# A graph attention layer on one core: the node phase's stores, the one-hot's place and the exponential steps

## The chip, the cores and the metric

The kernel runs on one core of a Trainium2 chip. The core has a matrix engine (TensorE, PE in the profile; PEld is its weight load), a vector engine (VectorE, DVE), a scalar engine (ScalarE, ACT), GpSimd (POOL) and a queue engine (SyncE, SP) that here only issues DMAs. The metric is the device time of one execution in microseconds (us); lower is better.

## The reference

There are 12500 nodes with 128 channels and 400000 edges, sorted by their target. What is computed:

```python
h = maximum(layernorm(x), 0)
msg_src = h @ w_src + b_src                    # per node
msg_dst = h @ w_dst
message = msg_src[edge_src] + msg_dst[edge_dst]   # per edge
rad_w = silu(silu(edge_attr_32 @ w1 + b1) @ w2 + b2) @ w3 + b3
message = message * edge_weight * rad_w
message = message @ w_sep + b_sep              # 8 heads of 16 alphas and 16 values
alpha, value = split(message)
score = einsum(smooth_leaky_relu(alpha), alpha_dot)       # per edge and head
att = segment_softmax(score, edge_dst)
out = segment_sum(value * att, edge_dst) @ w_proj + b_proj
return x + out
```

## The kernel before

**Node phase.** The nodes are taken in 25 groups, `Q`, twice. The first pass (`products(i, 0)`) makes rows `h @ w_src` and stores them to a table `t_src` in device memory; the second pass (`products(i, 1)`) makes `t_dst`. Between these products stand small jobs: layer norm statistics, the rows of the first five pairs (`raw_*`), and the loads of weights and of the first edges, which `weights_list()` hands to SyncE one or two at a time. `marks(j)` (L601) compares, on VectorE, each edge's target with the next one's and leaves a bf16 mark in `gt`; after the fourth quarter `same` is stored (L605 to L608), in device memory; later stages read it to see where a segment ends. Late in the second pass come the loads `load_d(0)`, `load_w(0)` and `load_w(1)`: targets and edge weights of the first pairs, into buffers of `messages`.

**Edge phase.** An edge section is 512 edges, and a *pair* is two sections, 1024 edges: 391 pairs. `windows()` runs `step(k)` for k = -5 to 390 and a tail; a step works on many pairs in different stages:

- GpSimd gathers the rows of `t_src` for pair k+2 with indirect DMAs of 128 rows (`gather`, L1111), eight per pair. The first five pairs are not gathered. GpSimd may run ahead of its step as far as buffers are free: pairs 5 to 12 go into `messages`, later ones into rotating buffers, six pairs deep (`gs`, `mT`, `xs`, `gu` are their names).
- The radial network runs three steps deep: `mlp1(k+2)` (PE L1127, ACT L1130, its two halves in the banks `m1` and `misc`), `mlp2(k+1)` (L1140, L1142), `mlp3(k)` (L1157) and `radial(k)` (DVE L1162, times the edge weight).
- `one_hot_T(k+1)` makes, on ACT (L1151, L1152), the one-hot of the targets, with which PE picks rows of `t_dst` (`md`, loaded by `load_md` at L1080, split by `split_md` into high and low parts on ACT L1090 and DVE L1094).
- `sources(k)` (PE L1173) transposes the gathered rows into the bank `pm`; `message(k)` (PE L1186) adds the target's part; DVE L1191 multiplies and leaves the message, `mT`.
- `alphas(k-1, f)` is PE's product L1197 and ACT's SiLU L1199, then DVE's L1204; `scores` (PE L1214, every second step) writes its result into `m1`.
- Every eighth step (k % 8 == 3, k = 11, 19, ... 387) is an *exponential step*: `softmax_exp` (ACT L1250) needs another function table in ACT than SiLU, so two table loads stand in it; `softmax_T` (PE L1284, ACT L1287) transposes the result through the bank `misc`.
- `values` (PE L1325, DVE L1327) and `sums` (PE L1340, L1352) work on pair k-12.

The order of the instructions on each engine is the order in which `step` calls these helpers; semaphores come from the framework's tracking of tiles. Each engine works its own list in order.

```python
for f in (1, 0):
    nc.scalar.activation(h1s[k][:, f, :], p1[f], AF.Silu, bias=b12[:, 0:1], scale=1.0)
```

Here `p1[0]` is `m1`, the bank that `scores` needs next in odd steps, and `p1[1]` is `misc`.

Of the kernel before, what the change touches and what calls it, by code (L numbers as in the profile page):

```python
# [42 lines left out]
KV = 320  # L43
MP = 8
# [3 lines left out]
AHEAD = 13  # L48
# [9 lines left out]
def gnn_kernel(ctx: ExitStack, tc: tile.TileContext, a: dict, out: bass.AP):  # L58
# [8 lines left out]
    NP = NS // 2  # L67
# [130 lines left out]
    with tc.tile_pool(name="node1", bufs=1) as n1, tc.tile_pool(name="node", bufs=2) as np_, \  # L198
# [80 lines left out]
        def weights_list():  # L279
# [10 lines left out]
            for f in range(2):  # L290
# [4 lines left out]
                for q in range(2):  # L295
# [4 lines left out]
                [lambda: load_d(0, early[AHEAD - 2].bitcast(I32).rearrange("p (n e) -> p n e", n=2)),  # L300
                 lambda: load_w(0, early[AHEAD - 3]), lambda: load_w(1, early[AHEAD - 1])]

# [334 lines left out]
        stats(*quads[4])  # L637
        roots(quads[3][0], quads[4][1])
        more = iter(weights_list())
        limits = load_limits()  # L640
        for i in range(Q):
# [31 lines left out]
            if i == 19:  # L673
                ends_load()
        extra = {7: lambda: (spans(), places()), 10: cuts, 12: direct_ids, 14: spreads,
                 15: lambda: marks(0), 16: lambda: marks(1), 18: lambda: marks(2), 20: lambda: marks(3)}
        for i in range(2 * RQ + 8):
            if i < Q:
                products(i, 1)
            if i % 2 == 0 and 0 <= i // 2 - 4 < RQ:  # L680
                raw_turn(i // 2 - 4)
            q = i // 2 - 1
            if i % 4 == 2 and q < RQ:
                raw_roots(q, q + 2)
            if i % 4 == 3 and q < RQ:
                raw_scales(q, q + 2)
            if i % 2 == 0 and 0 <= q - 1 < RQ:
                raw_norm(q - 1)
            if i in extra:
                extra[i]()  # L690
            load = next(more, None)
            if load:
                load()
            if i == 2 * RQ:
                nc.scalar.activation(silu, eps[0:1, :], AF.Silu)
# [313 lines left out]
    def windows():  # L1009
# [7 lines left out]
        with tc.tile_pool(name="ps", bufs=1, space=PSUM) as pp, \  # L1017
# [104 lines left out]
            def mlp1(k):  # L1122
# [5 lines left out]
                h1s[k] = sp.tile([P, 2, 2 * T], F32, name="h1")  # L1128
                for f in (1, 0):
                    nc.scalar.activation(h1s[k][:, f, :], p1[f], AF.Silu, bias=b12[:, 0:1], scale=1.0)  # L1130
# [506 lines left out]
            def has(k):  # L1637
                return 0 <= k < NP

            prep[0] = idx0  # L1640
            for k in range(2):
                load_md(k)

            def tail_head(c):
# [19 lines left out]
            def step(k):  # L1664
# [29 lines left out]
                if k % 16 == 7 and has(k + 9) and k > 7:  # L1694
                    prep_make((k + 9) // 16)
                if 0 <= k - 40 < 8:
                    padded_rows(k - 40)
                unit = k >= UNIT_STEP[0]
# [9 lines left out]
                if has(k + 1) and k >= 0:  # L1708
                    split_md(k + 1, 0)
                m, r = divmod(k, MP)  # L1710
                if k >= NP:
                    m, r = LAST_M + 1, k - NP
                if k == NP:
                    tail_head(c)
                    return
                if has(c):
                    weights(c)
                    values(c, 0)
# [10 lines left out]
                if has(k + 1) and k >= 0:  # L1729
                    split_md(k + 1, 1)  # L1730
                if has(k - 1):
# [6 lines left out]
                if has(k):  # L1738
                    mlp3(k)
                if has(k + 2):  # L1740
                    mlp1(k + 2)
                if has(k + 1):
                    one_hot_T(k + 1)
                if has(k):
                    radial(k)
                if k == 0:
                    for i in range(2):
                        split_md(0, i)
                if unit and q == 1:
# [29 lines left out]
                if has(k + 2):  # L1779
                    gather(k + 2, 1)  # L1780
                if has(k + 3):
                    e_T(k + 3)
# [10 lines left out]
                if has(k):  # L1793
                    message(k)
                if has(k - MP) and r == 3:
                    softmax_T(m - 1, 0)
# [229 lines left out]
```

## Time and profile before

| | |
|---|---|
| median of 3 runs | 4045.88 us (4044.23 to 4051.89) |
| profiled execution | 4045.58 us |
| its span, first to last instruction | 4043.7 us |
| mean granted TensorE clock | 0.974 |
| PE, DVE, ACT, POOL busy | 3734.2, 2966.2, 2317.5, 3015.5 us |

In the rows of a timeline the columns are the start in us, the duration in us, the engine, the line, the operation, output<-input tiles, and in brackets the idle time of the engine before it and what released it. In the rows of waits they are the total in us, the number of times and the longest. "issue" as a releaser means that the profile shows nothing that the engine waited for. SPq and POOLq rows are DMA issues. A granted clock of 0.50 means TensorE ran at half its speed in that stretch.

### The profile page before, as it was taken

What the parts mean: (1) busy time and instruction counts of PE and PEld (TensorE: products, weight loads), DVE (VectorE), ACT (ScalarE), POOL (GpSimd) and SP (SyncE); (2) the same over time, 40 slices, a digit from 0 to 9 for tenths busy, and PEclk for the clock granted to TensorE, in tenths of its full rate; (3) what the DMA queues carried; (4) which work ended last, traced back from release to release, by engine and by line L of the source; (5) the groups of instructions that cost most, each with busy time, mean ns of one, the idle gap of its engine ahead of it and who ended that gap; (6) DMA issues with size and microseconds to landing.
All of it is one profiled execution on the core that took longest, in us unless ns stands there. A gap on an engine that the chain in (4) does not pass through costs nothing. (4 is left out here: it accounts for less than half of the span.)

```text
span 4043.7 us, 82719 instructions
## 1 busy us (share of the span) xinstructions
PE 3734.2 (92%) x27186; PEld 2198.2 (54%) x27186; DVE 2966.2 (73%) x5236; ACT 2317.5 (57%) x4463; POOL 3015.5 (75%) x3193
## 2 busy tenths in 40 slices
PE   7699999999999999999999999999999999999997
PEld 6255555555555555555555555555555555565555
DVE  8477777777777767677777677777777777777876
ACT  7565555666655556555655565555555555555561
POOL 6767777777777777777777777777777777777776
PEclk9899999999999999999999999999999999999998
DMA  8756666666666665665566666666666666666662
GB/s 256 189 154 166 166 177 170 162 171 170 175 160 170 167 162 159 166 162 166 158 169 169 163 164 169 168 162 165 172 171 159 178 167 180 174 179 181 174 166 56
DMA packets 435839, 678.82 MB, mean 168 GB/s; under 512 B 96574, under 2 KB 268510, under 8 KB 435291
## 3 DMA queue, kind: packets, MB, share of 16 engines
q1 hardware_dynamic: 331931, 464.59, 39.4%
q0 software_dynamic: 101888, 207.34, 21.8%
q8 instruction: 220, 3.60, 0.4%
q14 instruction: 216, 1.77, 0.2%
q10 hardware_dynamic: 1584, 1.51, 0.1%
HBM read 620.73 MB, written 54.06 MB: 167 GB/s over the span
## 5 line engine op out<-in xcount | busy, mean ns | idle before, releaser
L1111 POOL DMA_INDIRECT gs<-t_src,idx x3013 | 2849.4, 946 | 932.4 <-issue 757.2
L1204 DVE SCALAR_TENSOR_TENSOR al<-pa,sl 128x512 f32<-128x512 f32 x781 | 538.9, 690 | 544.1 <-ACT sl L1199 533.2
L1197 PE MATMUL pa<-mT,c_w_a 128*128 128x512 f32 x1562 | 884.1, 648 | 38.7 <-DVE mT L1191 17.9
L1199 ACT ACTIVATE sl<-pa,c_b_a 128x512 f32<-128x512 f32 x781 | 536.8, 687 | 666.4 <-PE pa L1197 659.5
L1325 PE MATMUL V<-c_w_v,mT 128*128 128x128 f32 x6154 | 891.2, 288 | 11.4 <-DVE pvx L1327 10.7
L1325 PEld LDWEIGHTS V<-c_w_v,mT 128*128 128x128 f32 x6154 | 757.3, 194 | 240.9 <-issue 186.3
L1173 PEld LDWEIGHTS pm<-ident,gs 128*128 128x128 f32 x3013 | 374.5, 143 | 536.3 <-issue 526.3
L1142 ACT ACTIVATE h<-p,b 128x512 f32<-128x512 f32 x391 | 467.7, 1196 | 345.7 <-PE p L1140 339.5
L1327 DVE TENSOR_TENSOR pvx<-V,Pem 128x512 f32<-128x512 f32 x770 | 528.0, 686 | 146.4 <-PE V L1325 96.9
L1162 DVE SCALAR_TENSOR_TENSOR w_b<-p,c_fc_b,w_b 128x1024 f32<-128x1024 f32 x389 | 498.2, 1281 | 147.1 <-PE p L1157 119.7
L1173 PE MATMUL pm<-ident,gs 128*128 128x128 f32 x3013 | 464.3, 277 | 99.5 <-DMA gs<-t_src,idx 98.9
L1191 DVE SCALAR_TENSOR_TENSOR mT<-pm,c_b_src,w_b 128x1024 f32<-128x1024 f32 x389 | 495.6, 1274 | 14.8 <-PE pm L1186 14.5
L1130 ACT ACTIVATE h<-misc,b 128x256 f32<-128x256 f32 x391 | 185.6, 475 | 540.7 <-PE misc L1127 522.4
L1157 PE MATMUL p<-h,w3b 64*128 64x512 f32 x1564 | 454.9, 659 | 8.0 <-ACT h L1142 8.0
L1197 PEld LDWEIGHTS pa<-mT,c_w_a 128*128 128x128 f32 x1562 | 236.2, 191 | 288.3 <-issue 78.7
L1214 PE MATMUL m<-al,w_s 128*32 128x512 f32 x1564 | 215.8, 623 | 80.8 <-ACT h L1130 79.6
L1152 ACT ACTIVATE ohT<-d_b,ones 128x512 fp32r<-128x512 f32 x389 | 280.8, 722 | 13.0
L1151 ACT ACTIVATE d_b<-d_b,tgt 128x512 f32<-128x512 int32 x389 | 279.9, 719 | 0.0
L1140 PE MATMUL p<-h,w2b 64*64 64x256 f32 x3128 | 260.3, 403 | 0.0
L1127 PEld LDWEIGHTS m<-eT,w1b 64*128 64x128 f32 x782 | 151.0, 193 | 196.6 <-issue 169.9
L1127 PE MATMUL m<-eT,w1b 64*128 64x256 f32 x782 | 239.5, 387 | 3.9 <-DMA t_dst<-ms 2.7
L1127 PE MATMUL misc<-eT,w1b 64*128 64x256 f32 x782 | 239.5, 387 | 0.0
(257 smaller groups left out, 3730.3 us busy)
## 6 DMA issues: line engine op xcount, KB each, us to landing
w_b<-in_edge_weight SPq DMA_DIRECT2D x388, 512.0 KB
d_b<-in_dst SPq DMA_DIRECT2D x388, 256.0 KB
e_t<-in_edge_attr SPq DMA_DIRECT2D x381, 128.0 KB
gs<-t_src,idx POOLq DMA_INDIRECT x3013
md<-t_dst SPq DMA_DIRECT2D x782, 32.0 KB
win<-ob SPq DMA_DIRECT2D x230, 68.0 KB
agg<-ob SPq DMA_DIRECT2D x640, 16.5 KB
xs<-in_x SPq DMA_DIRECT2D x26, 256.0 KB
```

The lines of the kernel that those rows point to most:

```text
L1111: sent = [nc.gpsimd.indirect_dma_start(out=gs[:, t, :], out_offset=None, in_=t_src[:, :], in_offset=bass.IndirectOffsetOnAxis(ap=idx[:, t0 ...
L1127: nc.tensor.matmul(p1[f], w1b[s, :], eTs[k][s, :], start=True, stop=True)
L1142: nc.scalar.activation(h2s[k].rearrange("x (h i b) -> x h b i", h=2, b=2 * TS), p2[:, :, 0:2 * T].rearrange("x h (b i) -> x h b i", b=2 * TS),
L1157: nc.tensor.matmul(p3[:, f, 0:SEC], w3b[s, :], h2s[k][s, :], start=True, stop=True)
L1162: nc.vector.scalar_tensor_tensor(rad[:, 0:n], p3.rearrange("c f e -> c (f e)")[:, 0:n], b3, rad[:, 0:n], op0=ALU.add, op1=ALU.mult)
L1173: turned = [nc.tensor.matmul(pm[:, t * T:(t + 1) * T], gs[:, t, :], ident, start=(t == 0), stop=False, is_transpose=True, skip_group_check ...
L1191: nc.vector.scalar_tensor_tensor(mTs[k][:, 0:n], pms.rearrange("c f e -> c (f e)")[:, 0:n], b_n, rad[:, 0:n], op0=ALU.add, op1=ALU.mult)
L1197: nc.tensor.matmul(pa[:, 0:n], w_a, mTs[k][:, f * SEC:f * SEC + n], start=True, stop=True)
L1199: nc.scalar.activation(sl[:, 0:n], pa[:, 0:n], AF.Silu, bias=b_a, scale=1.0)
L1204: nc.vector.scalar_tensor_tensor(al, pa, 0.25, sl, op0=ALU.mult, op1=ALU.add)
L1325: nc.tensor.matmul(V[:, t, :], mTs[c][:, o:o + T], w_v, start=True, stop=True)
L1327: nc.vector.tensor_mul(pvx[c][:, f, 0:n, 0:C].rearrange("p t (h k) -> p t h k", h=H), V[:, 0:n, :].rearrange("p t (h k) -> p t h k", h=H), ...
```

## The change

Six things move; no operation of the computation is added or taken away.

1. `marks(0)` to `marks(3)`, and with them the stores of `same`, go from the second pass (groups 15, 16, 18, 20) into the last four groups of the first.
2. `load_w(1)`, the second pair's edge weights, goes from the node phase's list to just behind `load_md(0)` and `load_md(1)` at the start of `windows()`.
3. In odd `mlp1` up to pair 320, ACT reads `m1` first and `misc` second.
4. In step 0, pair 0's `split_md` stands where pair 1's stood, and pair 1's goes behind `message(0)`.
5. `one_hot_T(k+1)` goes from before `radial(k)` to behind the second `alphas` of the step.
6. In exponential steps `mlp1(k+2)` goes behind the second `alphas`, `sources` and `gather`.

Also, `padded_rows` is called in steps 40 to 51, two of every three, instead of 40 to 47. `raw_rows` is only a function around lines that were inline (its body and the removed lines are left out).

```diff
@@ -298,7 +298,7 @@
             return [lambda t=t, ap=ap: nc.sync.dma_start(out=t, in_=ap) for t, ap in pairs] + \
                 [lambda k=k: load_e(k, nc.sync) for k in range(4)] + \
                 [lambda: load_d(0, early[AHEAD - 2].bitcast(I32).rearrange("p (n e) -> p n e", n=2)),
-                 lambda: load_w(0, early[AHEAD - 3]), lambda: load_w(1, early[AHEAD - 1])]
+                 lambda: load_w(0, early[AHEAD - 3])]
 
 
         mv = n1.tile([P, NB, 3], F32, name="mv")
@@ -636,6 +636,18 @@
         stats(*quads[3])
         stats(*quads[4])
         roots(quads[3][0], quads[4][1])
...
         more = iter(weights_list())
         limits = load_limits()
         for i in range(Q):
@@ -672,20 +684,13 @@
                 ends_store()
             if i == 19:
                 ends_load()
-        extra = {7: lambda: (spans(), places()), 10: cuts, 12: direct_ids, 14: spreads,
-                 15: lambda: marks(0), 16: lambda: marks(1), 18: lambda: marks(2), 20: lambda: marks(3)}
+            if 0 <= i - (Q - 4) < 4:
+                marks(i - (Q - 4))
+        extra = {7: lambda: (spans(), places()), 10: cuts, 12: direct_ids, 14: spreads}
         for i in range(2 * RQ + 8):
             if i < Q:
                 products(i, 1)
...
+            raw_rows(i)
             if i in extra:
                 extra[i]()
             load = next(more, None)
@@ -1126,7 +1131,7 @@
                     s = slice(f * 2 * RAD, (f + 1) * 2 * RAD)
                     nc.tensor.matmul(p1[f], w1b[s, :], eTs[k][s, :], start=True, stop=True)
                 h1s[k] = sp.tile([P, 2, 2 * T], F32, name="h1")
-                for f in (1, 0):
+                for f in (0, 1) if k % 2 and k < KV else (1, 0):
                     nc.scalar.activation(h1s[k][:, f, :], p1[f], AF.Silu, bias=b12[:, 0:1], scale=1.0)
 
             def mlp2(k):
@@ -1640,6 +1645,7 @@
             prep[0] = idx0
             for k in range(2):
                 load_md(k)
+            load_w(1, early[AHEAD - 1])
 
             def tail_head(c):
 
@@ -1693,8 +1699,8 @@
                     prep_make(k // 2 - 1)
                 if k % 16 == 7 and has(k + 9) and k > 7:
                     prep_make((k + 9) // 16)
-                if 0 <= k - 40 < 8:
-                    padded_rows(k - 40)
+                if 0 <= k - 40 < 12 and (k - 40) % 3 != 1:
+                    padded_rows((k - 40) // 3 * 2 + (k - 40) % 3 // 2)
                 unit = k >= UNIT_STEP[0]
                 u = max((i for i, a in enumerate(UNIT_STEP) if a <= k), default=0)
                 q = k - UNIT_STEP[u]
@@ -1706,13 +1712,14 @@
                 if k % 16 == LAG - 1 and has(k - LAG + 1) and k < NP:
                     loc_turn(k // 16)
                 if has(k + 1) and k >= 0:
-                    split_md(k + 1, 0)
+                    split_md(k + (k > 0), 0)
                 m, r = divmod(k, MP)
                 if k >= NP:
                     m, r = LAST_M + 1, k - NP
                 if k == NP:
                     tail_head(c)
                     return
+                after = has(k - MP) and r == 3 and k < NP
                 if has(c):
                     weights(c)
                     values(c, 0)
@@ -1727,7 +1734,7 @@
                 if c - 2 >= D and has(c - 2):
                     direct_turn(c - 2)
                 if has(k + 1) and k >= 0:
-                    split_md(k + 1, 1)
+                    split_md(k + (k > 0), 1)
                 if has(k - 1):
                     alphas_sum(k - 1, 0, *sl)
                 j, o = divmod(k - LATE, SB)
@@ -1737,15 +1744,10 @@
                         block_exp(j)
                 if has(k):
                     mlp3(k)
-                if has(k + 2):
+                if has(k + 2) and not after:
                     mlp1(k + 2)
-                if has(k + 1):
-                    one_hot_T(k + 1)
                 if has(k):
                     radial(k)
-                if k == 0:
-                    for i in range(2):
-                        split_md(0, i)
                 if unit and q == 1:
                     unit_bias(u)
                     unit_quotients(u, sp)
@@ -1778,6 +1780,10 @@
                     sources(k, 1)
                 if has(k + 2):
                     gather(k + 2, 1)
+                if has(k + 2) and after:
+                    mlp1(k + 2)
+                if has(k + 1):
+                    one_hot_T(k + 1)
                 if has(k + 3):
                     e_T(k + 3)
                 if has(k - 1):
@@ -1792,6 +1798,9 @@
                     direct_out(c - 2)
                 if has(k):
                     message(k)
+                if k == 0:
+                    for i in range(2):
+                        split_md(1, i)
                 if has(k - MP) and r == 3:
                     softmax_T(m - 1, 0)
                 if has(k + 1):
```

Where it moves instructions, first on SyncE. Before, this is the end of its list for the node phase; `mT` are the buffers of `messages` that take targets and weights:

```order
L605 DMA same<-gt 96x3584
L605 DMA same<-gt 15x3584
L607 DMA same<-gt 1x2176
L608 DMA same<-past 1x1409
L175 DMA e_t<-in_edge_attr 128x256
L367 DMA t_dst<-ms_1223 128x1024
L187 DMA mT<-in_dst 64x2x512 x2
L194 DMA mT<-in_edge_weight 128x1024
L367 DMA t_dst<-ms_1257 128x1024
L194 DMA mT<-in_edge_weight 128x1024
L367 DMA t_dst<-ms_1282 128x128
L369 DMA t_dst<-ms_1282 84x128
```

After the change the same end reads as follows, in the same place:

```order
L367 DMA t_dst<-ms_1194 128x1024
L175 DMA e_t<-in_edge_attr 128x256 x2
L367 DMA t_dst<-ms_1228 128x1024
L187 DMA mT<-in_dst 64x2x512 x2
L194 DMA mT<-in_edge_weight 128x1024
L367 DMA t_dst<-ms_1257 128x1024
L367 DMA t_dst<-ms_1281 128x128
L369 DMA t_dst<-ms_1281 84x128
```

The four stores of `same` and one of the two weight loads are gone from it. The stores stand now between the last store of `t_src` and the first of `t_dst`, some thirty rows further up:

```order
L367 DMA t_src<-ms_872 128x128
L369 DMA t_src<-ms_872 84x128
L298 DMA c_fc_w_146<-in_fc_w 64x128
L605 DMA same<-gt 96x3584
L605 DMA same<-gt 15x3584
L607 DMA same<-gt 1x2176
L608 DMA same<-past 1x1409
L298 DMA c_fc_b_147<-in_fc_b 128x1
L367 DMA t_dst<-ms_888 128x1024
```

And the second pair's weights stand behind the `md` loads of pairs 0 and 1:

```order
L1082 TENSOR_LOAD base x2
L1085 ISA
L1085 DMA md<-t_dst 64x1x128
L1085 ISA
L1085 DMA md<-t_dst 64x1x128
L194 DMA mT<-in_edge_weight 128x1024
L1082 TENSOR_LOAD base x2
L1085 ISA
```

They are the next thing on SyncE after those four loads of `md`.

On ACT, an odd step of the first ten, before (`h` are `mlp1`'s halves, `d_b` and `ohT` the one-hot, `sl` the alphas' SiLU):

```order
L1199 ACTIVATE sl<-pa,c_b_a 128x512
L1130 ACTIVATE h_1718<-misc,b_131 128x256
L1130 ACTIVATE h_1718<-m_1333,b_131 128x256
L1151 ACTIVATE d_b<-d_b,tgt 128x512
L1152 ACTIVATE ohT<-d_b,ones 128x512
L1199 ACTIVATE sl<-pa,c_b_a 128x512
L1142 ACTIVATE h_1753<-p_1332,b_131 128x2x8x32
```

The same rows after:

```order
L1204 ACTIVATE sl<-pa,c_b_a 128x512
L1135 ACTIVATE h_1718<-m_1332,b_131 128x256
L1135 ACTIVATE h_1718<-misc,b_131 128x256
L1204 ACTIVATE sl<-pa,c_b_a 128x512
L1156 ACTIVATE d_b<-d_b,tgt 128x512
L1157 ACTIVATE ohT<-d_b,ones 128x512
L1147 ACTIVATE h_1753<-p_1331,b_131 128x2x8x32
```

The second `sl` is now ahead of the one-hot instead of behind it, and the half of `h` from the bank `m` is made first.

Step 19, an exponential step, on ACT, before (`Pr` is the exponential, `S` the scores' copy, `Pem` the transposes' copies):

```order
L1250 ACT_TABLE_LOAD
L1250 ACTIVATE Pr<-M 128x512
L1130 ACT_TABLE_LOAD
L1130 ACTIVATE h_2916<-misc,b_131 128x256
L1130 ACTIVATE h_2916<-m_1333,b_131 128x256
L1151 ACTIVATE d_b<-d_b,tgt 128x512
L1152 ACTIVATE ohT<-d_b,ones 128x512
L1218 ACTIVATE S<-m_1333,b_s 128x512
L1199 ACTIVATE sl<-pa,c_b_a 128x512
L1287 COPY Pem<-misc 128x256
L1142 ACTIVATE h_2964<-p_1332,b_131 128x2x8x32
```

And after:

```order
L1255 ACT_TABLE_LOAD
L1255 ACTIVATE Pr<-M 128x512
L1223 ACTIVATE S<-m_1332,b_s 128x512
L1204 ACT_TABLE_LOAD
L1204 ACTIVATE sl<-pa,c_b_a 128x512
L1135 ACTIVATE h_2943<-m_1332,b_131 128x256
L1135 ACTIVATE h_2943<-misc,b_131 128x256
L1156 ACTIVATE d_b<-d_b,tgt 128x512
L1157 ACTIVATE ohT<-d_b,ones 128x512
L1292 COPY Pem<-misc 128x256
L1147 ACTIVATE h_2964<-p_1331,b_131 128x2x8x32
```

Both have two table loads; the second stood ahead of `mlp1`'s SiLUs and now stands behind `S`, ahead of the alphas' SiLU. The same step on PE, before:

```order
L1157 MATMUL p_1332<-h_3691,w3b 128x512 x2
L1127 MATMUL m_1333<-eT,w1b 128x256
L1127 MATMUL misc<-eT,w1b 128x256
L1325 MATMUL V<-c_w_v,mT 128x128 x4
L1214 MATMUL m_1333<-al,w_s_170 32x512 x4
L1197 MATMUL pa<-mT,c_w_a 128x512
L1173 MATMUL pm<-ident,gs_3567 128x128 x4
L1186 MATMUL pm<-ohT,m_3604 128x512 x2
L1284 MATMUL misc<-ident,Pr 128x128 x2
L1140 MATMUL p_1332<-h_3634,w2b 64x256 x4
L1284 MATMUL misc<-ident,Pr 128x128 x2
```

And after:

```order
L1162 MATMUL p_1331<-h_3691,w3b 128x512 x2
L1330 MATMUL V<-c_w_v,mT 128x128 x4
L1219 MATMUL m_1332<-al,w_s_170 32x512 x4
L1202 MATMUL pa<-mT,c_w_a 128x512
L1178 MATMUL pm<-ident,gs_3564 128x128 x4
L1132 MATMUL m_1332<-eT,w1b 128x256
L1132 MATMUL misc<-eT,w1b 128x256
L1191 MATMUL pm<-ohT,m_3604 128x512 x2
L1289 MATMUL misc<-ident,Pr 128x128 x2
L1145 MATMUL p_1331<-h_3634,w2b 64x256 x4
L1289 MATMUL misc<-ident,Pr 128x128 x2
```

The two products of `mlp1` (L1127, now L1132) moved from in front of `values` and the scores to behind the alphas and the sources, and stand ahead of the first transposes through `misc`.

More of the change, by code (lines that the diff above doesn't have):

```diff
@@ L638, in gnn_kernel, with raw_rows @@
         roots(quads[3][0], quads[4][1])
+        def raw_rows(i):
+            if i % 2 == 0 and 0 <= i // 2 - 4 < RQ:
+                raw_turn(i // 2 - 4)
+            q = i // 2 - 1
+            if i % 4 == 2 and q < RQ:
+                raw_roots(q, q + 2)
+            if i % 4 == 3 and q < RQ:
+                raw_scales(q, q + 2)
+            if i % 2 == 0 and 0 <= q - 1 < RQ:
+                raw_norm(q - 1)
         more = iter(weights_list())
@@ L679, in gnn_kernel @@
                 products(i, 1)
[L680 to L688, printed above, removed]
+            raw_rows(i)
             if i in extra:
```

## The prediction

> **What bounds the kernel now.** I read the page first, then the waits of POOL and PE, then POOL's timeline. The page's busy shares and its costliest group:
>
> ```profile
> PE 3734.2 (92%) x27186; PEld 2198.2 (54%) x27186; DVE 2966.2 (73%) x5236; ACT 2317.5 (57%) x4463; POOL 3015.5 (75%) x3193
> ...
> L1111 POOL DMA_INDIRECT gs<-t_src,idx x3013 | 2849.4, 946 | 932.4 <-issue 757.2
> ```
>
> PE at 92% looks like the bound and POOL at 75% does not. But POOL's idle time is named "issue". The waits of POOL over the span, then the row of L1173 between 320 and 3951 us (columns: total, times, longest):
>
> ```profile
> POOL gs L1111 <- issue: 757.2, 2484, 0.3
> ```
> ```profile
> POOL gs L1111 <- PE pm L1173: 29.3, 96, 0.3
> ```
>
> No gap in that stretch is longer than 0.3 us, whatever is named as its releaser: POOL never waits for a buffer there. A gather costs 0.946 busy + 0.30 issue = 1.25 us, eight per pair, 10.0 us per pair. POOL's timeline, at the first gather, the three that stood out, and the last:
>
> ```profile
> 72.19 0.94 POOL L1111 DMA_INDIRECT mT<-t_src,idx  x1 [11.84 <-DMA c_fc_b<-in_fc_b]
> 129.77 0.94 POOL L1111 DMA_INDIRECT mT<-t_src,idx  x1 [5.03 <-DVE mT L1191]
> 237.32 0.94 POOL L1111 DMA_INDIRECT gs<-t_src,idx  x1 [7.98 <-PE pm L1173]
> 303.39 0.94 POOL L1111 DMA_INDIRECT gs<-t_src,idx  x1 [6.38 <-PE pm L1173]
> 3950.24 0.94 POOL L1111 DMA_INDIRECT gs<-t_src,idx  x1 [0.30 <-PE misc L1352]
> ```
>
> From 72.19 to 3951.18 us the gathers are one queue, with three waits in it. So the end of the kernel is the start of that queue, plus 3085 x 1.25 us (400000 edges by 128, less 40 of the raw pairs), plus those waits, plus 92.5 us of tail. PE, for its part, waits for gathers through the run (span; then 2670 to 3940 us):
>
> ```profile
> PE pm L1173 <- DMA gs<-t_src,idx: 98.9, 80, 4.6
> PE m L1214 <- ACT h L1130: 79.6, 45, 2.9
> ```
> ```profile
> PE pm L1173 <- DMA gs<-t_src,idx: 30.0, 26, 4.2
> ```
>
> What PE saves after the last POOL wait at 303 us only lengthens its 98.9 us of waiting for gathers. The 79.6 us that the scores (L1214) wait for ACT are therefore no gain as such. A gain has to come out of POOL's waits: 5.03 + 7.98 + 6.38 less 3 x 0.30 of issue = 18.5 us.
>
> Four gathers were also slow, under the four marks on DVE. The first and last of them, and one mark:
>
> ```profile
> 91.15 1.42 POOL L1111 DMA_INDIRECT mT<-t_src,idx  x1 [0.30 <-issue]
> ...
> 97.91 1.86 POOL L1111 DMA_INDIRECT mT<-t_src,idx  x1 [0.30 <-issue]
> ```
> ```profile
> 90.67 1.08 DVE L601 TENSOR_TENSOR gt<-cur 112x896 bf16<-112x896 int32 x1
> ```
>
> The others took 1.55 and 1.63 us; over 0.945 each, the four lost 2.7 us. The cap of what POOL can give is 18.5 + 2.7 = 21.2 us. The waits are for buffers that pairs 0, 13 and 20 have to leave, so POOL gains only as far as these pairs get earlier: x, the lead of the sources of pair 20, decides. **POOL's gain is the smaller of x and 21.2.**
>
> **The change part by part.** First the node phase's end (SyncE's issues, then ACT, then two windows: length, busy time of PE, PEld, DVE, ACT and POOL, granted clock, DMA share, GB/s; last a wait of ACT):
>
> ```profile
> 98.98 0.88 SPq L605 DMA_DIRECT2D same<-gt  x2
> ...
> 106.04 1.12 SPq L194 DMA_DIRECT2D mT<-in_edge_weight  x1
> 107.26 0.70 SPq L367 DMA_DIRECT2D t_dst<-ms  x1
> ```
> ```profile
> 95.57 0.30 ACT L392 ACTIVATE rstdr<-mvr,eps 128x8 f32<-128x8 f32 x1 [2.08 <-DVE mvr L390]
> ...
> 117.17 0.47 ACT L1130 ACTIVATE h<-misc,b 128x256 f32<-128x256 f32 x1 [8.61 <-DMA t_dst<-ms]
> ...
> 124.44 0.40 ACT L1090 ACTIVATE m<-md,sign 128x128 fp32r<-128x128 f32 x1 [4.00 <-DMA md<-t_dst]
> ...
> 126.84 0.39 ACT L1090 ACTIVATE m<-md,sign 128x128 fp32r<-128x128 f32 x1
> ```
> ```profile
> 72.00:98.00 26.00, 19.99 (x145) 18.17 (x145) 22.10 (x86) 14.71 (x35) 20.02 (x20) 0.87 0.74 246
> 98.00:117.00 19.00, 9.25 (x37) 4.79 (x35) 4.42 (x8) 6.37 (x15) 14.73 (x15) 0.60 0.93 286
> ```
> ```profile
> ACT h L1130 <- DMA mT<-in_dst: 4.2, 1, 4.2
> ```
>
> Between 98 and 117 us the DMA engines are 93% busy at 286 GB/s, and the first steps stand until t_dst has landed (117.17). The marks' stores (about 784 KB) and the second pair's weights (512 KB) lie in that stretch, ahead of the last t_dst stores: 1.33 MB / 286 GB/s = 4.6 us, in which SyncE's issue times lie too. Both are taken out: the marks' stores go to about 70 us, the weights behind the md loads. The four marks leave the second pass (4 x 1.08 us on DVE). DVE is waited for there only in part (2.08 us at 95.57); I put 1.1 us net, since the first pass ends about as much later. T(t_dst) comes earlier by 4.6 + 1.1, rounded to **6.0**; ends: 0 if the stores that moved push the second pass's start as much, 7 if issue and bytes partly add. The start of the gathers is bound by t_src's last store on SyncE, ahead of which nothing is added: 0 to +0.3, taken as 0. What the weights wait for next: pair 1 needs them one step later, behind 2 md loads; cover is that step of 9 us against a transfer of 512 KB, 2 us.
>
> In step 0 the split of pair 0 now goes first. It stood at 126.84, behind pair 1's at 124.44 and two SiLUs and the one-hot: **2.4** earlier. Step 1 gets up to 0.9 more out of the 4.2 that ACT waited there on a d load, since the first SiLU no longer stands behind it; taken **0.9** (0 to 0.9).
>
> Steps 2 to 10 next; step 6 stands for the even, 185.70 for the odd ones (ACT, DVE, PE):
>
> ```profile
> 177.68 0.72 ACT L1151 ACTIVATE d_b<-d_b,tgt 128x512 f32<-128x512 int32 x1
> 178.43 0.72 ACT L1152 ACTIVATE ohT<-d_b,ones 128x512 fp32r<-128x512 f32 x1
> 179.06 0.67 ACT L1199 ACTIVATE sl<-pa,c_b_a 128x512 f32<-128x512 f32 x1
> ...
> 182.87 0.69 ACT L1199 ACTIVATE sl<-pa,c_b_a 128x512 f32<-128x512 f32 x1 [1.91 <-PE pa L1197]
> ```
> ```profile
> 179.76 0.69 DVE L1204 SCALAR_TENSOR_TENSOR al<-pa,sl 128x512 f32<-128x512 f32 x1 [1.61 <-ACT sl L1199]
> ```
> ```profile
> 176.84 1.12 PE L1197 MATMUL pa<-mT,c_w_a 128*128 128x512 f32 x2
> ...
> 181.70 1.12 PE L1197 MATMUL pa<-mT,c_w_a 128*128 128x512 f32 x2 [2.29 <-DVE mT L1191]
> ...
> 185.70 1.06 PE L1214 MATMUL m<-al,w_s 128*32 128x512 f32 x8 [0.94 <-ACT h L1130]
> ```
>
> The chain is SiLU, al (DVE), message mT (DVE), PE. The SiLU stands behind the one-hot; PE's product pa (issued 176.84, 1.12 long) was done at 177.96, so with the one-hot behind it the SiLU starts 1.05 earlier, and PE's 2.29 us wait shrinks by that: 5 x 1.05 = 5.25. In odd steps the scores need the bank that ACT read second; the new order frees it one SiLU of 0.37 sooner: 4 x 0.37 = 1.5. Sum **6.75** (0 to 9). The one-hot itself is needed a step later: hidden by the 1.91 us that ACT idles at 182.87; with that cover gone it would cost the SiLU there up to 1.44. Spreading the padded rows over steps 40 to 51 falls behind 303 us, where POOL has no wait left to shorten: 0.
>
> Exponential steps 11 and 19 lie ahead of the third wait. Step 19 (ACT, PE, and a window with the granted clock):
>
> ```profile
> 292.85 1.28 ACT L1130 ACT_TABLE_LOAD   x1
> ...
> 296.25 0.67 ACT L1218 ACTIVATE S<-m,b_s 128x512 f32<-128x512 f32 x1
> ```
> ```profile
> 291.49 0.38 PE L1127 MATMUL m<-eT,w1b 64*128 64x256 f32 x1
> ...
> 292.02 1.16 PE L1325 MATMUL V<-c_w_v,mT 128*128 128x128 f32 x8
> 295.04 1.07 PE L1214 MATMUL m<-al,w_s 128*32 128x512 f32 x8 [1.86 <-ACT h L1130]
> ...
> 302.52 0.60 PE L1173 MATMUL pm<-ident,gs 128*128 128x128 f32 x4
> ```
> ```profile
> 296.30:299.70 3.40, 3.40 (x10) 1.50 (x9) 0.85 (x2) 1.31 (x3) 0.71 (x1) 0.50 0.41 105
> ```
>
> Before: scores wait 1.86 for two SiLUs behind two table loads (the second shown), then PE runs 3.4 us at a granted clock of 0.50. After: without mlp1 (291.49 to 292.02) ahead, the values run at 291.5 to 292.6, the scores at once to 293.6; ACT then does S to 294.3, the second table load to 295.5, the late SiLU to 296.2, mlp1's two to 297.1. The transposes (L1284) wait for mlp1's bank until 297.1 and again behind the one-hot and a copy until 298.8; values and alphas follow, and pair 20's sources start at about 301.2 instead of 302.5: **1.25** each (0 to 2), twice, **2.5**. The second load is not gone, it is late next, ahead of the SiLU.
>
> In the window just shown the clock stands at 0.50 right after a wait of 1.86 us. The Trainium skill ("TensorE: Matmul & The Clock Gate", What's actually happening) lets the clock drop only after an idle window of about 3.4 us; this trace does not agree with it, so I leave the new waits of about 1.1 us a chance to cost clock, and put it in the range of 0 to 2. By the page they could not, and each exponential step would give nearer 2, the total 1.5 us more.
>
> x = 6.0 + 2.4 + 0.9 + 6.75 + 2.5 = 18.55, below the cap of 21.2. POOL gains 18.55. The last exponential step, 387, may lengthen or shorten the tail: -1.5 to +1.5, taken 0. The profiled execution took 4045.58 us (span 4043.7 and 1.9 around it), 0.3 from the median of 4045.88. 4045.58 - 18.55 = **4027.0**; own range 4022 to 4032.
>
> **The rivals.** 0.2%, 8 us, is about what a measurement of this kernel tells from no change.
> 1. The stores at 70 us hold the second pass up by as much as they free later (for: the DMA engines are 74% busy from 72 to 98 us; against: DVE is busy 22.10 of those 26 us, so the stage goes by DVE, and it loses the marks). The term 6.0 falls to 0: x = 12.55, 4033.
> 2. The exponential steps give nothing, the clock still halves after two short waits, the late load hits the tail: 18.55 - 2.5 - 1.5 = 14.5, 4031.
> 3. The waits stay for another reason, such as the second weights landing late and holding message 1, now that they are issued after t_dst's landing: the 6.0, the 2.4 and the 0.9 are lost and some of the rest, x of 4 to 8, about 4040.
> 4. Slower: one mechanism, the exponential step grows. If the second load and the one-hot ahead of the copies cost more than the wait removed, PE becomes the bound. PE's whole reserve is the 98.9 us; with 48 exponential steps (11, 19, ... 387) a growth g each makes the end later by 48 g - 98.9. It eats the 18.55 and 8 more at g = (98.9 + 26.55) / 48 = 2.6 us. Working through step 19 gives -1.25, and I find no row for +2.6.
> 5. PE is the bound after all, and the 79.6 us of scores' waits go: 3966. Against it stand POOL's 0.3 us gaps over 3600 us.
>
> **How the numbers follow.** Forecast 0.60, rival 1 0.14, rival 2 0.12, rival 3 0.08, rival 4 0.04, rival 5 0.02. Faster: 0.60 + 0.14 + 0.12 + 0.02, 0.87 with a part taken off for the edges; same 0.09 (rival 3 and edges); slower 0.04. The range reaches from the cap with a good tail and the scatter of runs (4045.6 - 21.2 - 1.5 - 4, 4019, put at 4018) to rival 3's better half, 4040.
>
> **What would show it.** Right: POOL waits at pair 10 gone or nearly, at pair 20 gone, at pair 26 about 3 us; the four slow gathers at 0.94; t_dst's wait on ACT ending near 111; PE's waits for gathers up by 50 to 80 us while the scores' waits fall. Wrong: a POOL gap over 0.3 us after 310 us, a first gather later than 73, or steps between two exponential ones whose PE no longer waits for gathers.

## The result, and the profile after

| | before | after |
|---|---|---|
| median of 5 runs | 4047.99 us (4044.23 to 4051.89) | 4026.9 us (4025.19 to 4030.34) |
| span of the profiled execution | 4043.7 us | 4024.0 us |
| mean granted TensorE clock | 0.974 | 0.982 |

The ratio is 0.9952, 95% interval 0.9939 to 0.9964: faster by 0.5%. The forecast was 4027.0 us. (Eleven of the twelve runs in the experiments below fell on occasions on which the kernel before, too, took 5488 to 5681 us; they are called disturbed, and each is compared only with runs of its own occasion.)

The page after, its busy shares and the costliest group:

```profile
PE 3725.5 (93%) x27186; PEld 2195.9 (55%) x27186; DVE 2967.6 (74%) x5236; ACT 2273.4 (56%) x4463; POOL 3015.5 (75%) x3193
...
L1116 POOL DMA_INDIRECT gs<-t_src,idx x3013 | 2850.5, 946 | 922.7 <-issue 769.3
```

Little there tells that the kernel got faster: POOL's busy time is the same to 0.1 us, and PE's fell by 8.7. What moved is in POOL's timeline. The first gather after, the only two gaps over 0.35 us, and the last gather:

```profile
70.88 1.28 POOL L1116 DMA_INDIRECT mT<-t_src,idx  x1 [9.36 <-DMA c_fc_w<-in_fc_w]
285.28 0.94 POOL L1116 DMA_INDIRECT gs<-t_src,idx  x1 [4.42 <-PE pm L1178]
290.42 0.94 POOL L1116 DMA_INDIRECT gs<-t_src,idx  x1 [0.45 <-PE pm L1178]
3933.22 0.94 POOL L1116 DMA_INDIRECT gs<-t_src,idx  x1 [0.31 <-issue]
```

The waits at pairs 10 and 20 (5.03 and 7.98 us) are gone; the one at pair 26 is 4.42 instead of 6.38. The gather of pair 26 starts 303.39 - 285.28 = 18.1 us earlier, and the last gather ends at 3934.16 instead of 3951.18, 17.0 earlier. From 320 to 3935 us POOL again waits for nobody longer than 0.3 us; the row of its waits for the sources:

```profile
POOL gs L1116 <- PE pm L1178: 20.7, 68, 0.3
```

PE's waits after, over the span:

```profile
PE pm L1178 <- DMA gs<-t_src,idx: 113.9, 88, 4.3
PE misc L1289 <- ACT h L1135: 37.7, 43, 1.2
PE misc L1289 <- ACT Pem L1292: 32.1, 49, 1.0
...
PE m L1219 <- ACT h L1135: 2.2, 4, 0.6
```

The scores' 79.6 us of waiting fell to 2.2. In their place stand 37.7 + 32.1 = 69.8 us of waiting in front of the transposes of the exponential steps (L1289), first for `mlp1`'s SiLUs to leave the bank `misc`, then for the copy out of it.

### The profile page after: what moved, and what is told of

It is laid out like the page before. It is cut to its first block, busy times and chain, and to the rows that moved or that the text cites. A ratio compares the mean times of both kernels' runs of the same rounds, so it can differ in the third digit from the quotient of the medians.

```text
span 4024.0 us, 82582 instructions
## 1 busy us (share of the span) xinstructions
PE 3725.5 (93%) x27186; PEld 2195.9 (55%) x27186; DVE 2967.6 (74%) x5236; ACT 2273.4 (56%) x4463; POOL 3015.5 (75%) x3193
## 5 line engine op out<-in xcount | busy, mean ns | idle before, releaser
L1116 POOL DMA_INDIRECT gs<-t_src,idx x3013 | 2850.5, 946 | 922.7 <-issue 769.3
L1178 PEld LDWEIGHTS pm<-ident,gs 128*128 128x128 f32 x3013 | 369.9, 142 | 554.0 <-issue 545.6
L1178 PE MATMUL pm<-ident,gs 128*128 128x128 f32 x3013 | 461.0, 276 | 115.9 <-DMA gs<-t_src,idx 113.9
L1135 ACT ACTIVATE h<-m,b 128x256 f32<-128x256 f32 x391 | 183.2, 469 | 163.1 <-PE misc L1132 157.6
L1132 PE MATMUL misc<-eT,w1b 64*128 64x256 f32 x782 | 243.3, 392 | 4.6 <-DVE oh L1317 4.5
L1132 PE MATMUL m<-eT,w1b 64*128 64x256 f32 x782 | 243.4, 392 | 2.8 <-DVE eT L1125 1.8
L1132 PEld LDWEIGHTS m<-eT,w1b 64*128 64x128 f32 x782 | 146.5, 192 | 178.9 <-issue 161.8
```

Source lines behind the costliest of these rows:

```text
L1116: sent = [nc.gpsimd.indirect_dma_start(out=gs[:, t, :], out_offset=None, in_=t_src[:, :], in_offset=bass.IndirectOffsetOnAxis(ap=idx[:, t0 ...
L1132: nc.tensor.matmul(p1[f], w1b[s, :], eTs[k][s, :], start=True, stop=True)
L1178: turned = [nc.tensor.matmul(pm[:, t * T:(t + 1) * T], gs[:, t, :], ident, start=(t == 0), stop=False, is_transpose=True, skip_group_check ...
```

## The experiments

Two theories. G: the gather queue paces; only the lead that PE has gained when pair 20's rows are freed reaches the end. P: PE paces, and what its steps save counts wherever they stand.

**What the three undisturbed traces say themselves.** The lead of the changed kernel, by the start of a pair's sources on PE (L1173 before, L1178 after). Pair 20 before is in the prediction (302.52). Pairs 54 and 110 before:

```profile
630.60 0.60 PE L1173 MATMUL pm<-ident,gs 128*128 128x128 f32 x4
```
```profile
1153.33 0.60 PE L1173 MATMUL pm<-ident,gs 128*128 128x128 f32 x4
```

Pairs 20, 54 and 110 after:

```profile
284.41 0.60 PE L1178 MATMUL pm<-ident,gs 128*128 128x128 f32 x4
```
```profile
597.33 0.60 PE L1178 MATMUL pm<-ident,gs 128*128 128x128 f32 x4
```
```profile
1135.66 0.52 PE L1178 MATMUL pm<-ident,gs 128*128 128x128 f32 x3 [2.48 <-DMA gs<-t_src,idx]
```

Pair 20 leads by 302.52 - 284.41 = 18.1 us, pair 54 by 630.60 - 597.33 = 33.3, pair 110 by 1153.33 - 1135.66 = 17.7, and the last gather by 17.0. PE won 15 us more between pairs 20 and 54 and gave all of it back by pair 110, where it stands waiting for a gather. That is what G says and not what P says.

**Seven gather buffers and an earlier load (label both).** This run and its kernel before were undisturbed.

```diff
-GSB = 6
+GSB = 7
...
             load_w(1, early[AHEAD - 1])
+            load_d(1, lp.tile([P, 2, SEC], I32, name="d_b"))
...
-                if k % 2 and k >= -1 and has(k + 3):
+                if k % 2 and k >= 1 and has(k + 3):
                     load_d((k + 3) // 2, lp.tile([P, 2, SEC], I32, name="d_b"))
...
-                    load_w(k + 2, lp.tile([P, PR], F32, name="w_b", bufs=3))
...
                 if has(k):
                     message(k)
+                if has(k + 2) and k >= 0:
+                    load_w(k + 2, lp.tile([P, PR], F32, name="w_b", bufs=2))
```

> The changed kernel with seven gather buffers (two instead of three buffers of edge weights, their load issued behind the step's message) and with the second pair of pairs' targets loaded ahead of the step loop. If the gather queue paces: its last wait, 4.4 us at pair 26, and the 0.45 behind it go, no wait is left in the queue, and the time falls by 4.5 us from the changed kernel's, about 25 from the kernel before. If two buffers make the weights late, the radial product waits for them in every step and the time grows by tens of us. If PE paces: no change against the changed kernel.

Measured: 4030.16 us (4028.48 to 4031.84, 4 runs) against 4053.25 of the kernel before (7 runs) on that chip, ratio 0.9945 (0.9928 to 0.9962). The waits of POOL for the sources, the first and the last gather, and the group of gathers:

```profile
POOL gs L1116 <- PE pm L1178: 23.5, 77, 0.3
```
```profile
71.23 0.95 POOL L1116 DMA_INDIRECT mT<-t_src,idx  x1 [9.70 <-DMA c_fc_w<-in_fc_w]
```
```profile
3936.25 0.94 POOL L1116 DMA_INDIRECT gs<-t_src,idx  x1 [0.30 <-issue]
```
```profile
L1116 POOL DMA_INDIRECT gs<-t_src,idx x3013 | 2857.2, 948 | 918.8 <-issue 769.0
```

No wait is left in the whole queue, as G said. The two buffers of weights held DVE up only twice, by 0.77 us at 134.55 and by 2.39 at 143.51. But the last gather ends at 3937.19, 3.0 us later than in the changed kernel: in this execution the 3013 gathers took 2857.2 us instead of 2850.5, 6.7 us more. A queue that starts 0.35 us later and takes 6.7 us longer, less about 4.3 us for the waits that are gone, should end 2.8 us later, and so it does within 0.3: the queue passes the longer gathers on. They are longer evenly (the median gather took 947 ns instead of 944); whether that comes from the occasion or from this version is not shown. The kernel before was also 5.3 us slower on this chip (4053.25 against 4047.99). Measured against its own kernel before, the version saves 23.1 us, the change 21.1; the intervals overlap, so that it beats the changed kernel is not shown. Its queue is the shorter one by its waits; nothing more is left to win there with buffers.

The earlier `load_d(1)` did remove ACT's wait for it at 128.58 (below), and another came up, for `md`:

```profile
125.63 0.40 ACT L1095 ACTIVATE m<-md,sign 128x128 fp32r<-128x128 f32 x1 [4.03 <-DMA md<-t_dst]
```

The sources of pair 5 came 1.2 us earlier than in the changed kernel (155.47 against 156.71).

**The parts, on the disturbed occasions.** In these runs engines stood for long without a wait that the profile can name. The start of the run "early" on PE, and POOL's longest group of waits in "exp27":

```profile
23.11 2.08 PE L353 MATMUL pm<-w_src,x_all 128*128 128x128 f32 x8 [3.59 <-issue]
...
40.55 2.07 PE L353 MATMUL pm<-w_src,x_all 128*128 128x128 f32 x8 [14.51 <-issue]
```
```profile
POOL gs L1111 <- PE pm L1173: 1075.2, 255, 66.4
```

PE stood 14.5 us for nothing that the profile shows, 26 us into the run. That its instructions came late is the likeliest reading, but no run shows it. Further on POOL waits 1075 us for PE's sources, against 44.4 in the undisturbed kernel before: there the gather queue does not pace, so these runs cannot decide between G and P for the undisturbed kernel. What each gave is told for that.

Late `mlp1` alone, in steps behind the last wait, and in steps 11 and 19 alone; the marks alone; the second weights alone:

```diff
+                after = has(k - MP) and r == 3 and k < NP and k >= 27    # exp11_19: k < 27
-                if has(k + 2):
+                if has(k + 2) and not after:
                     mlp1(k + 2)
...
                     gather(k + 2, 1)
+                if has(k + 2) and after:
+                    mlp1(k + 2)
```

> The kernel before with the late first MLP layer only in exponential steps 27, 35, ... 387, behind the last wait of the gather queue. If the gather queue paces: its waits at pairs 10, 20 and 26 stay at 5.0, 8.0 and 6.4 us, PE waits some 50 us more for gathers, and the span stays within 3 us of 4043.7. If PE paces: some 1.6 us less in each of about 40 steps, a span near 3980.

> The kernel before with the late first MLP layer only in exponential steps 11 and 19. If the gather queue paces: the sources of pair 13 come 2.7 us earlier and those of pair 20 4.3 us, so the wait at pair 20 falls from 8.0 to 5.3 and that at pair 26 from 6.4 to 4.8, and the span falls by about 4.3 us. If PE paces: two steps of 46, no more than 4 us at once and none left at the end, where PE waits for gathers.

```diff
+            if 0 <= i - (Q - 4) < 4:          # marks
+                marks(i - (Q - 4))
-                 15: lambda: marks(0), 16: lambda: marks(1), 18: lambda: marks(2), 20: lambda: marks(3)}
...
-                 lambda: load_w(0, early[AHEAD - 3]), lambda: load_w(1, early[AHEAD - 1])]     # w1
+                 lambda: load_w(0, early[AHEAD - 3])]
...
+            load_w(1, early[AHEAD - 1])       # behind load_md(0), load_md(1)
```

> The kernel before with the marks and their stores in the first pass, nothing else. The prediction's bytes: 784 KB at 286 GB/s is 2.7 us, and 1.1 from the work taken out of the second pass, so ACT's wait for t_dst ends 3.8 us earlier than 117.17, the slow gathers at 91 to 98 us are gone, and the span falls by about 4. If the stores only push the second pass back: ACT's wait ends at 117 and the span stays.

> The kernel before with the second pair's weights behind the first md loads, nothing else. By bytes: 512 KB at 286 GB/s is 1.8 us; by the issue and the lanes on SyncE up to 3. ACT's wait for t_dst ends 2 to 3 us earlier than 117.17, and the span falls by as much. If the weights then land too late for pair 1: its radial waits and the lead is gone by the message of pair 1.

One run each: 5609.71 (exp27), 5547.07 (exp11_19), 5515.54 (marks) and 5603.71 us (w1), against one of 5488.18. The kernel before alone lies anywhere between 5488 and 5681 us in its runs on such occasions, 193 us apart, and the largest of these differences is 122, so none can be told from no difference. All four are inconclusive.

The one-hot and the SiLU order alone, on the kernel before; one gather more in every eighth pair, and one product more in every fourth step, on the changed kernel; seven gather buffers without the earlier load (its diff stands above):

```diff
-                if has(k + 1):               # onehot
-                    one_hot_T(k + 1)
...
                     gather(k + 2, 1)
+                if has(k + 1):
+                    one_hot_T(k + 1)
...
-                for f in (1, 0):
+                for f in (0, 1) if k % 2 and k < KV else (1, 0):
```

> The kernel before with the one-hot behind the second alphas and the first MLP layer's SiLUs in the order m1, misc in odd steps, nothing else. Steps 2 to 10 by the prediction's count: 6.75 us of lead at the sources of pair 11; by what the changed kernel showed, 0.4 and 1.05 in turn from pair 5 on, 4.3 to 6.7. The span falls by the lead that is left at pair 20, 4 to 7 us.

```diff
+                if f == 1 and k % 8 == 4 and 32 <= k < 384:      # extra_gather
+                    dup = lp.tile([P, C], F32, name="dup", bufs=1)
+                    nc.gpsimd.indirect_dma_start(out=dup, out_offset=None, in_=t_src[:, :],
+                        in_offset=bass.IndirectOffsetOnAxis(ap=idx[:, t0:t0 + 1], axis=0))
```

> The changed kernel with one gather more, into a tile that nothing reads, in every eighth pair from 36 to 380: 44 of 1.25 us. If the gather queue paces: the span grows by 55 us, and PE's waits for gathers by about as much. If PE paces: POOL has 25% idle time, and the span stays at 4024.

```diff
-                nc.tensor.matmul(pa[:, 0:n], w_a, mTs[k][:, f * SEC:f * SEC + n], start=True, stop=True)
+                for _ in range(2 if k % 4 == 1 and f == 1 and 32 <= k < 376 else 1):      # extra_pe
+                    nc.tensor.matmul(pa[:, 0:n], w_a, mTs[k][:, f * SEC:f * SEC + n], start=True, stop=True)
```

> The changed kernel with one alphas product made twice in every fourth step from 33 to 373: 86 products of about 0.5 us, 43 us of TensorE work. If the gather queue paces: PE's waits for gathers fall from 114 to about 70 us and the span stays within 3 us of 4024. If PE paces: a span near 4067.

> The changed kernel with seven instead of six gather buffers; room is made by two instead of three buffers of edge weights, whose load is issued behind the step's message. If the gather queue paces: its last wait, 4.4 us at pair 26, and the 0.45 behind it go, and the span falls by 4.5 us to about 4019.5. If the weights' load comes late with two buffers, the radial product waits for it in every step, and the span grows by tens of us. If PE paces: no change.

5491.83, 5645.0, 5614.29 and 5533.03 us, against one run of 5613.64: inconclusive for the same reason. The last one is the changed kernel with late `mlp1` only in steps 11 and 19:

```diff
-                after = has(k - MP) and r == 3 and k < NP
+                after = has(k - MP) and r == 3 and k < 27
```

> The changed kernel with the late first MLP layer only in exponential steps 11 and 19; steps 27 to 387 stand as in the kernel before. If the gather queue paces: the wait at pair 26 is again the only one of the queue, at 4.4 us, the 43 later exponential steps lose their 1.6 us against PE's waits for gathers, which fall by some 50 us, and the span stays within 3 us of 4024. If PE paces, it goes up by some 70 us, past the kernel before.

5381.6 against 5563.54 us, one run each: 182 us less, still within those 193.

The two halves of the change with intervals: node_exp27 joins the diffs of the marks, the second weights, late `mlp1` from step 27, and pair 0's split first; steps_gather joins those of the one-hot, late `mlp1` in steps 11 and 19, and the added gathers.

> The kernel before with the node phase's part of the change (marks and their stores early, second weights late, pair 0's split first) and the late first MLP layer only in exponential steps 27 to 387, behind the queue's last wait. If the gather queue paces: the sources of pair 5 lead by about 9.3 us, those of pairs 13 and 20 by no more; the queue's wait at pair 10 goes, those at pairs 20 and 26 stay near 7.5 and 6.4 us, and the time falls by 9 to 12 us (the lead and up to 2.7 of tail). The 46 late steps give nothing but longer waits of PE for gathers. If PE paces: they give about 1.6 us each, and the time falls by 60 us or more.

> The kernel before with the other part of the change (one-hot behind the second alphas, SiLU order, late first MLP layer in exponential steps 11 and 19) and with one gather more, into a tile that nothing reads, in every eighth pair from 36 to 380: 44 of 1.25 us. If the gather queue paces: the sources of pair 11 lead by 4.3 to 6.75 us and those of pair 20 by 8.6 to 11; the wait at pair 10 stays at 5.0, that at pair 20 falls below 1.5, that at pair 26 to about 4.8; the added gathers cost 55 us in full, so the time grows by 44 to 46 us less up to 2.7 of tail. If PE paces: POOL idles for a quarter of the span and hides them, and the time stays or falls by 4.

Measured against the same 11 runs of the kernel before, median 5634.62 us: node_exp27 5675.62, ratio 1.01 (1.0044 to 1.0157); steps_gather 5570.84, ratio 0.9892 (0.9861 to 0.9922). POOL's waits for PE, in this order:

```profile
POOL gs L1112 <- PE pm L1174: 1074.7, 255, 67.4
```
```profile
POOL gs L1111 <- PE pm L1178: 847.7, 231, 61.6
```

Neither theory's number came; both were worked out from undisturbed traces. With POOL waiting 848 us for PE, the run with 44 more gathers was not 44 to 46 us longer but 64 us shorter. That fits a POOL that has time to spare there, but the same run also moved the one-hot, so what the 44 gathers alone cost is not shown. In the undisturbed kernel, 6.7 us of longer gathers went into the end of the queue. The wait of POOL for PE is what tells the two conditions apart. Which part of node_exp27 made it slower was not tried.

## Why the prediction was right, point by point

**The pacer.** Right: the leads above, and the queue's end 17.0 us earlier for 18.1 at pair 20. The missing 1.1 us is gathers that ran a little longer (2850.5 against 2849.4 us). This rests on the traces; no single part was undone in the undisturbed condition. By place the 18.1 us of x are 9.3 up to pair 5, 4.3 from there to pair 11, 2.7 in step 11, 0.2 behind it and 1.6 in step 19. The terms missed on both sides, as told below; that the median came out 0.1 us from the forecast is luck.

**The term of t_dst, 6.0.** ACT after, from t_dst's landing on:

```profile
110.39 0.47 ACT L1135 ACTIVATE h<-m,b 128x256 f32<-128x256 f32 x1 [5.49 <-DMA t_dst<-ms]
...
116.77 0.40 ACT L1095 ACTIVATE m<-md,sign 128x128 fp32r<-128x128 f32 x1 [3.12 <-issue]
...
128.58 0.72 ACT L1156 ACTIVATE d_b<-d_b,tgt 128x512 f32<-128x512 int32 x1 [2.56 <-DMA d_b<-in_dst]
```

117.17 became 110.39: 6.8 us. But some of it was there long before anything that the change moves. A load that stands in the same place in both kernels let DVE go on 1.15 us earlier, before and after:

```profile
37.82 0.28 DVE L256 COPY ends<-cur 112x7 int32<-112x7 int32 x2 [2.66 <-DMA cur<-in_dst]
```
```profile
36.67 0.26 DVE L256 COPY ends<-cur 112x7 int32<-112x7 int32 x2 [1.52 <-DMA cur<-in_dst]
```

The version with seven buffers has the earlier time too (36.66); why the load lands earlier is open. That leaves some 5.6 us for the moves, near 6.0. The forecast priced most of it by bytes. SyncE's last store of t_dst, before and after, says that 5.7 of the 6.8 us were there when it was issued, and only 1.1 came between issue and landing:

```profile
108.06 0.75 SPq L369 DMA_DIRECT2D t_dst<-ms  x1
```
```profile
102.35 0.84 SPq L369 DMA_DIRECT2D t_dst<-ms  x1
```

So the size was near and its working is not borne out as far as the bytes go. How it divides between the stores, the marks and the weights is open.

**Step 0, 2.4, and step 1, 0.9.** The first message ended at 120.69 instead of 129.50, so 8.8 - 6.8 = 2.0 are left for the split, near 2.4. The 0.9 of step 1 rests on a misread row, for the 4.2 us wait stands ahead of t_dst's landing, before:

```profile
107.72 0.47 ACT L1130 ACTIVATE h<-misc,b 128x256 f32<-128x256 f32 x1 [4.17 <-DMA mT<-in_dst]
```

Behind it ACT waited for t_dst until 117.17 anyway, so it had nothing to give. The second message was still ready 11.3 us earlier (139.18 to 127.93): step 1 gave about 2.4, as ACT's wait ahead of the third pair's split fell from 3.15 us (at 133.17) to 0.99 (at 122.41). Then the prediction missed a wait: at 128.58 ACT stands 2.56 us for the second targets, whose load is not earlier by as much. At the sources of pair 5 the lead is 165.98 - 156.71 = 9.3 us. That equals 6.0 + 2.4 + 0.9 only by chance: by the forecast steps 2 to 4 should have added another 2.5 by then.

**Steps 2 to 10, 6.75.** Mis-sized: from pair 5 to pair 11 the lead grows from 9.3 to 13.6 us, by 4.3. The sources of these two pairs, before and then after:

```profile
165.98 0.60 PE L1173 MATMUL pm<-ident,mT 128*128 128x128 f32 x4
...
215.99 0.60 PE L1173 MATMUL pm<-ident,mT 128*128 128x128 f32 x4
```
```profile
156.71 0.60 PE L1178 MATMUL pm<-ident,mT 128*128 128x128 f32 x4
...
202.40 0.60 PE L1178 MATMUL pm<-ident,mT 128*128 128x128 f32 x4
```

Step for step the lead grows by 0.4 and 1.05 in turn, the sizes that were worked out; but that holds for six steps. In steps 2 to 4 the lead fell from 11.3 to 9.3 us, with the wait for the targets among them.

**Exponential steps, 1.25 each.** Step 11 gave 2.7, more than the range of 0 to 2, and step 19 gave 1.6. The order of events was right, and what it gives was not. Step 19 after, on PE:

```profile
276.15 1.07 PE L1219 MATMUL m<-al,w_s 128*32 128x512 f32 x8
277.15 1.13 PE L1202 MATMUL pa<-mT,c_w_a 128*128 128x512 f32 x2
278.11 0.60 PE L1178 MATMUL pm<-ident,gu 128*128 128x128 f32 x4
...
280.76 0.44 PE L1289 MATMUL misc<-ident,Pr 128*128 128x128 f32 x2 [1.18 <-ACT h L1135]
...
282.38 0.44 PE L1289 MATMUL misc<-ident,Pr 128*128 128x128 f32 x2 [0.59 <-ACT Pem L1292]
```

The same two products before:

```profile
296.03 1.88 PE L1197 MATMUL pa<-mT,c_w_a 128*128 128x512 f32 x2
297.71 1.06 PE L1173 MATMUL pm<-ident,gu 128*128 128x128 f32 x4
```

The waits come in the predicted order. But they are 1.18 + 0.59 = 1.77 us against 1.86 before: the chain is hardly shorter. What is gone is the half clock: pa took 1.13 instead of 1.88, the sources 0.60 instead of 1.06. The kernel before has the same short step where its clock stays. Its step 43, on PE:

```profile
526.51 1.07 PE L1214 MATMUL m<-al,w_s 128*32 128x512 f32 x8 [1.72 <-ACT h L1130]
527.50 1.13 PE L1197 MATMUL pa<-mT,c_w_a 128*128 128x512 f32 x2
```

That step took 10.94 us from sources to sources, and step 19 after 10.93. And the changed kernel has the long one where the clock drops; step 59:

```profile
652.33 1.92 PE L1330 MATMUL V<-c_w_v,mT 128*128 128x128 f32 x8
654.04 1.84 PE L1202 MATMUL pa<-mT,c_w_a 128*128 128x512 f32 x2
```

That step took 12.59 us. What decides can be read from the trace. From 140 us on the stretches at half clock begin on a grid of 3.413 us (before at 221.17, 296.27, 371.36, 446.45 and 504.48: 22, 22, 22 and 17 grid steps apart), and most of them last one grid step. Four grid steps, with length, busy time of PE, PEld, DVE, ACT and POOL, clock, DMA share and GB/s: before in steps 19 and 43, then after in steps 59 and 19.

```profile
292.85:296.27 3.42, 1.56 (x12) 0.53 (x12) 2.14 (x5) 3.37 (x6) 2.51 (x4) 1.00 0.54 104
524.96:528.37 3.41, 1.86 (x10) 0.59 (x11) 2.01 (x5) 3.36 (x6) 2.50 (x4) 1.00 0.61 126
```
```profile
648.84:652.26 3.42, 1.65 (x16) 0.64 (x13) 1.89 (x2) 3.38 (x8) 2.51 (x3) 1.00 0.40 107
280.20:283.61 3.41, 2.26 (x21) 1.64 (x22) 1.69 (x2) 3.38 (x8) 0.66 (x1) 1.00 0.47 131
```

After 1.56 and 1.65 us of PE work the next grid step ran at 0.50; after 1.86 and 2.26 it ran at full clock. So what counts here is whether PE was busy for about half of a grid step, and thus how the waits fall on the grid. Moving `mlp1` turned one wait into two as long in sum with work between them, which more seldom lie in one grid step: from sources to sources, 20 of the 48 exponential steps hold a stretch at half clock before and 10 after. For two single steps that is partly luck. The prediction had put the clock into the range (0 to 2) and not into the term. Step 11 before also ran at half clock (from 221.17), and its old wait was longer, 2.94 us, hence 2.7.

**The tail, 0 (-1.5 to +1.5).** Out of its bounds: from the last gather to the end 4024.0 - 3934.16 = 89.8 us instead of 92.5. POOL's stores there, before and after:

```profile
3999.57 1.01 POOL L1405 DMA_INDIRECT out<-gs,ids_d  x1 [11.64 <-DVE dq L1384]
4026.82 0.97 POOL L1405 DMA_INDIRECT out<-gs,ids_d  x1 [0.69 <-DVE rr L1844]
4030.74 0.97 POOL L1405 DMA_INDIRECT out<-gs,ids_d  x1 [1.67 <-DVE gs L1398]
```
```profile
3981.09 1.01 POOL L1410 DMA_INDIRECT out<-gs,ids_d  x1 [10.20 <-DMA win<-ob]
4011.04 0.97 POOL L1410 DMA_INDIRECT out<-gs,ids_d  x1 [0.70 <-DVE gs L1403]
```

1.5 us went ahead of the first of these stores (48.4 us after the last gather before, 46.9 after), and the rest behind it, where one wait of 1.67 is gone. The version with seven buffers has a tail of 4026.3 - 3937.19 = 89.1, so the shorter tail is not one execution's alone; which part of the change does it is open. Against the sum, x gained 0.4 us less, the gathers took 1.1 more and the tail gave 2.7: 17.0 + 2.7 = 19.7 us of span against 18.55.

**The first gather** came 1.3 us earlier (70.88), where 0 to +0.3 later was forecast; 1.15 of it is the load at 36.67. The queue's earlier start bought nothing by itself: pair 26's wait took it up, which is most of why that wait is 4.4 and not 3.

**What would show it.** Most came as written: the two waits gone, the slow gathers at 91 to 98 us gone, t_dst near 111, the scores' waits down. Pair 26's wait was 4.4 and not 3, and PE's waits for gathers did not rise by 50 to 80 us but by 15.0, since most of the scores' wait had turned into the transposes' and not into time saved.

## What to carry to other kernels

Look for the queue that never waits before counting what the busiest engine could save: here POOL at 75%, whose idle time is all issue, carried the end, and of a change spread over 4000 us only what happened in the first 303 counted. Follow each buffer wait of that queue back to the step that frees the buffer, and count the lead there, term by term; look in each step for the load that is late next. And when a wait moves, add up the waits after it as well before booking a gain, and look whether it is the wait or the clock behind it that costs the time.

## What the runs showed of the hardware

- The clock drop does not go by the length of a wait alone. From 140 us on in the three undisturbed traces the granted clock changed on a fixed grid of 3.413 us. Of the 99 grid steps at full clock in which PE was busy for less than half, 87 were followed by one at 0.50; of the 3199 others, 11 were. So a wait of 1.86 us halved the clock (step 19 before) and one of 1.72 us, of which 1.55 lay in one grid step, did not (step 43). The two lengths of an exponential step that come back most often, 10.9 and 12.5 us, differ by that; others lie between and beyond them.
- A gather's mean length differed from one undisturbed trace to another: 2849.4, 2850.5 and 2857.2 us for the 3013, each of another kernel, and on a queue that paces that is 8 us of the time, as much as 0.2% of it.
- On some occasions the same kernel takes 5488 to 5681 us instead of 4044 to 4060. The profile names no wait for part of that ("issue", on PE up to 14.5 us at a time within the first 45 us of the run "early"); the cause is not shown.
